# A graph network on one core: the second convolution for the two chosen experts only, rows ordered by expert

## The chip, the core and the metric

The kernel runs on one core of a Trainium2 chip. The metric is device time in microseconds (us), measured over whole executions. The profile is one execution recorded by the hardware profiler. In it TensorE is PE (its weight loads PEld), VectorE is DVE, ScalarE is ACT, GpSimd is POOL, and SyncE is SP, which only issues DMAs. Lines such as L1417 are lines of the kernel before.

## What is computed

A graph of N = 10,000 nodes with 512 features has E = 160,000 edges, sorted by destination. Layer 0 is a mixture of four experts, each made of two graph convolutions. Layer 1 is graph attention with a feed-forward part. The change is in layer 0, cut here to what matters:

```python
gates = softmax(x @ gate_W + gate_b)
top_v, top_i = top_k(gates, 2)                  # two of four experts for each node
def sage_conv(h, W_l, b_l, W_r):
    aggr = segment_sum(h[src], dst) * inv_deg   # mean over the incoming edges
    return aggr @ W_l + b_l + h @ W_r
for e in range(4):
    h = x
    for l in range(2):
        h = relu(sage_conv(h, Wl[e, l], bl[e, l], Wr[e, l]))
    expert_outs.append(h)
out = sum(take_along_axis(stack(expert_outs), top_i) * top_v)
x = layernorm(x + out)                          # then layer 1: q, k, v, attention, feed-forward
```

A node uses only the outputs of its two chosen experts, but a node's first convolution is needed for any expert that one of its neighbours along an edge has chosen.

## The kernel before, in words

Nodes are cut into 79 blocks of 128, and a block into four windows of 32 destinations. Each window has 5 slots of 128 edges (`CAP` 5), so a block has 20 gathers. A gather is an indirect DMA that POOL issues: one row of a table for each of 128 edges. PE adds the rows up with a one-hot matrix, 32 destination columns at a time, four windows side by side. A round is one slot of all four windows.

**Stage 1** (72 to 3992 us of the span) takes the blocks in pairs. `gather` sums the rows of `x`; `turned` transposes sums and own rows; `conv` (L1181 to L1191) computes the first convolution of all four experts with the weights held still and 256 nodes streaming; `products` (L1193 to L1203) multiplies the result at once with the second convolution's `Wl` (`wn`) and stores it, four experts in eight places a row, in `y_tab`. The eight places hold every pair of experts side by side, so that one gather later brings both chosen rows (1,024 numbers). The activations themselves go to `h_tab`.

Beside that, `side` drives two generators. `plan_src`, on DVE, works out where each edge goes in a table sorted by source for layer 1: 158 counting steps, 158 scanning steps (L969 to L972) and some closing ones. `scatter_src` then sends the edges there, 1,250 indirect DMAs from POOL (L1057). Stage 1's order on PE, DVE, ACT and POOL is written out by hand, so each of these engines does its instructions in the order of the code.

**Stage 2** (3992 to 6991) takes the blocks one by one. `pull` (L1319 to L1326) gathers the pairs of rows into a ring of 12 tiles (`YB`, the tiles `ring` and `y`). `rounds` sums them into two PSUM tiles `p_ag`, one for each chosen expert (L1417). `own` (L1368) multiplies the block's activations with `Wr` of all four experts, adds the bias with a bf16 product of ones and rows, and picks with masks (L1378 to L1385). The two are joined, passed through Relu with the gate as scale, and added to `x`; then come the norm and `project`, which makes q, k and v (L1340). Four and three scatters of the edge table stand in each block. PE and POOL are ordered by hand here, the other engines by the scheduler.

**Stage 3** (6991 to the end) is attention and feed-forward.

A last check adds up flags in `fail`; where one is set (too many edges in a window, for example), a slow general version runs instead.

Of the kernel before, what the change touches and what calls it, by code (L numbers as in the profile page):

```python
# [8 lines left out]
F32 = mybir.dt.float32  # L9
# [611 lines left out]

SPREAD = 60.0
# [12 lines left out]
def fast(ctx: ExitStack, tc: tile.TileContext, a: dict, out: bass.AP, bad: bass.AP):  # L635
# [23 lines left out]
    NPR = NW // 2  # L659
    assert E % P == 0 and E >= SL and NP <= SKIP_ROW and NPR <= 256  # L660

# [14 lines left out]
    fail = consts.tile([P, 4], F32, name="fail")  # L676
# [7 lines left out]
    y_tab = dram.tile([NP, NS, D], F32, name="y_tab")  # L684
    h_tab = dram.tile([NSB, P, NE, KD, 2 * P], F32, name="h_tab")
# [3 lines left out]
    wqkv_s = dram.tile([3, P, KD, D], F32, name="wqkv_s")  # L689
    fold_s = dram.tile([3, D], F32, name="fold_s")  # L690
    rows_s = dram.tile([3, NE + 5, D], BF16, name="rows_s")
# [23 lines left out]
    def split_rows(full, mine, part, i, v, add):  # L715

        nc.sync.dma_start(full, bass.AP(tensor=v.tensor, offset=v.offset, ap=[[0, 3], [1, D]]))
        if add is not None:
            nc.sync.dma_start(mine, add.partition_broadcast(3))
            nc.vector.tensor_add(full, full, mine)  # L720
# [20 lines left out]
    def normed(pool, src, name):  # L741
# [9 lines left out]
        t = pool.tile([P, D], F32, name=name)  # L751
# [6 lines left out]
    gate_w = mp.tile([P, NB, NE], F32, name="gate_w")  # L758
# [7 lines left out]
    empty = mp.tile([P, FC, WP], F32, name="empty")  # L766

    def fill_slots():
        nc.gpsimd.memset(empty, 0.0)
        nc.gpsimd.memset(empty.bitcast(I32)[:, :, 0:1], SKIP_ROW)  # L770
        nc.gpsimd.memset(empty[:, :, 1:2], FAR)
        yield
        for c0 in range(0, NC, FC):
            n = min(FC, NC - c0)
            nc.sync.dma_start(slots1[:, c0:c0 + n, :], empty[:, :n, :])
            yield
# [3 lines left out]
    wn = [wp.tile([P, KD, D], F32, name=f"wn{e}") for e in range(NE)]  # L780
    wr = big[4:7] + [wp.tile([P, KD, D], F32, name="wr3")]
    wl = big[:4]
    nc.gpsimd.memset(ring, 0.0)
# [5 lines left out]
    for w, n in zip(wn, "qkv"):  # L789
        load_to(w, a[f"L1_gnn_W{n}_T"], nc.scalar)  # L790
# [3 lines left out]
    def fold(pool, ps):  # L794
        off = pool.tile([1, D], F32, name="off")
        for i, w in enumerate(wn[:3]):
# [8 lines left out]
            nc.scalar.dma_start(wqkv_s[i], w)  # L805
# [80 lines left out]
    bl = wp.tile([P, NE, KD], F32, name="bl")  # L886
    for e in range(NE):
        nc.sync.dma_start(bl[:, e, :], a["L0_gnn_bl"][e, 0].rearrange("(k p) -> p k", p=P))
    for e in range(NE):
        load_to(wn[e], a["L0_gnn_Wl"][e, 1])  # L890
# [173 lines left out]

    def drive(gen, n):
# [4 lines left out]

    at512 = mp.tile([P, NB], F32, name="at512")
    pick = mp.tile([P, 2, NB, NE], F32, name="pick")
    gsel = mp.tile([P, 2, NB], F32, name="gsel")
# [35 lines left out]


    with p1, tc.tile_pool(name="p1k", bufs=1) as kp, tc.tile_pool(name="p1", bufs=2) as dp, \
# [3 lines left out]
        GB = 10  # L1115
        gbuf = [ring[:, i * D:(i + 1) * D] for i in range(GB)]

        def pull(i):

            b, k = divmod(i, BC)  # L1120
            if b < NB:
                c, j = divmod(k, NQ)
                nc.gpsimd.indirect_dma_start(  # L1123
                    out=gbuf[i % GB], out_offset=None, in_=x,
# [13 lines left out]
        def gather(s, rows):  # L1138

            rounds = [(b, c) for b in SB[s] for c in range(CAP)]  # L1140
            for r, (b, c) in enumerate(rounds):
# [4 lines left out]
                for j in range(NQ):  # L1146
                    i = (b * CAP + c) * NQ + j
                    nc.tensor.matmul(p_ag[j * W:(j + 1) * W, :], oh[:, j * CAP + c, :],  # L1148
                                     gbuf[i % GB], start=(c == 0), stop=(c == CAP - 1))
                for j in range(NQ):  # L1150
                    pull((b * CAP + c) * NQ + j + GB)
# [13 lines left out]
                if r % 2:  # L1165
                    yield
# [7 lines left out]
        def turned_all(rows):  # L1174
            tt = dp.tile([P, 2, KD, 2 * P], F32, name="tt", bufs=1)
# [5 lines left out]
        def conv(tt, e, n):  # L1181
            h = dp.tile([P, KD, 2 * P], F32, name="h", bufs=4)
            for f in range(KD):
                ph = pm.tile([P, D], F32, name="mm")
                for i, w in enumerate((wl[e], wr[e])):
                    for k in range(KD):
                        nc.tensor.matmul(ph[:, :n], w[:, k, f * P:(f + 1) * P], tt[:, i, k, :n],  # L1187
                                         start=(i + k == 0), stop=(i == 1 and k == KD - 1))
                nc.scalar.activation(h[:, f, :n], ph[:, :n], AF.Relu, bias=bl[:, e, f:f + 1])  # L1189
                side(e, f)  # L1190
            return h  # L1191

        def products(s, h, e, n):  # L1193
            for i, b in enumerate(SB[s]):
                py = pm.tile([P, D], F32, name="mm")
                for k in range(KD):
                    nc.tensor.matmul(py, h[:, k, i * P:(i + 1) * P], wn[e][:, k, :],  # L1197
                                     start=(k == 0), stop=(k == KD - 1))
                y = dp.tile([P, D], F32, name="y")
                nc.scalar.copy(y, py)  # L1200
                for at in [k for k in range(NS) if SEQ[k] == e]:
                    nc.sync.dma_start(y_tab[b * P:(b + 1) * P, at, :], y)
            nc.sync.dma_start(h_tab[s, :, e, :, :n], h[:, :, :n])  # L1203

        fill = fill_slots()
        plan = plan_src(kp, pm)
        scat = scatter_src(mp)
        planned, planning = [], [0]

        def side(e, f):  # L1210

            if planned:
                drive(scat, 2 if f < KD - 1 else 1)
            elif f < KD - 1 or e % 2:
                counted = planning[0] > NPR
                for _ in range(1 if counted else 4):
# [7 lines left out]
        vectors = [(a["L0_gnn_bl"][e, 1], None) for e in range(NE)] \  # L1224
            + [(a[f"L1_gnn_b{n}"], fold_s[i]) for i, n in enumerate("qkv")] \
# [700 lines left out]
```

## Time and profile before

| | |
|---|---|
| median of 10 runs | 10,061.99 us (10,054.58 to 10,071.37) |
| the profiled execution | 10,060.42 us |
| its span | 10,058.6 us |
| PE busy | 9,435.7 us, 94% |
| POOL busy | 6,876.2 us, 68% |
| DVE busy | 5,289.6 us, 53% |
| ACT busy | 3,010.8 us, 30% |
| first convolution, PE (L1187, first group) | 8,960 instructions |
| `products`, PE (L1197) | 2,528 instructions |
| `own`, PE (L1378) | 2,528 instructions |
| gathers of stage 1 (L1123) | 1,580 |
| gathers of stage 2 (L1323) | 1,580 |
| scatters of the edge table (L1057) | 1,250 |

An fp32 product is two PE instructions in the trace. Busy times of lines that overlap on PE cannot be added; the lengths of stretches in the timeline can. Issuing an ordinary DMA is not counted as busy time of an engine, but an indirect DMA is busy time of POOL while POOL prepares it; the gap in front of it is listed as idle, with what ended it. "issue" there means that the engine waited for nothing the profile shows.

### The profile page before, as it was taken

What the parts mean: (1) busy time and instruction counts of PE and PEld (TensorE: products, weight loads), DVE (VectorE), ACT (ScalarE), POOL (GpSimd) and SP (SyncE); (2) the same over time, 40 slices, a digit from 0 to 9 for tenths busy, and PEclk for the clock granted to TensorE, in tenths of its full rate; (3) what the DMA queues carried; (4) which work ended last, traced back from release to release, by engine and by line L of the source; (5) the groups of instructions that cost most, each with busy time, mean ns of one, the idle gap of its engine ahead of it and who ended that gap; (6) DMA issues with size and microseconds to landing.
All of it is one profiled execution on the core that took longest, in us unless ns stands there. A gap on an engine that the chain in (4) does not pass through costs nothing.

```text
span 10058.6 us, 169077 instructions
## 1 busy us (share of the span) xinstructions
PE 9435.7 (94%) x63887; PEld 5512.0 (55%) x63887; DVE 5289.6 (53%) x8244; ACT 3010.8 (30%) x5827; POOL 6876.2 (68%) x6736
## 2 busy tenths in 40 slices
PE   7999999999999998999999999998888888888888
PEld 4666666666666665333333333333555555555555
DVE  7898891000000012334333443344888888888885
ACT  1111111111111111111111111111566666666665
POOL 5566666777777774777777777776766666666664
PEclk9999999999999999999999999999999999999999
DMA  6544455455554554888888888886788877887874
GB/s 212 178 154 157 158 160 161 155 161 156 164 167 153 162 156 145 274 293 293 293 296 299 291 293 301 292 296 227 252 255 256 255 250 256 254 254 253 255 256 129
DMA packets 1076313, 2256.12 MB, mean 224 GB/s; under 512 B 250459, under 2 KB 500214, under 8 KB 1074720
## 3 DMA queue, kind: packets, MB, share of 16 engines
q0 software_dynamic: 588224, 1654.56, 51.0%
q1 hardware_dynamic: 479546, 576.99, 17.0%
q10 hardware_dynamic: 7718, 13.65, 0.4%
q8 instruction: 508, 8.32, 0.3%
q14 instruction: 317, 2.60, 0.1%
HBM read 2174.00 MB, written 378.96 MB: 254 GB/s over the span
## 4 chain that ended last, share of the span: by engine, by line
PE 71%; DVE 12%; DMA 8%; ACT 5%; issue 3%; POOL 1%; POOLq 0%; ACTq 0%; DVEq 0%; SPq 0%
PE mm L1187 20%; PE mm L1378 10%; PE mm L1197 10%; PE mm L1340 6%; PE p_ag L1417 6%; PE p_ag L1148 3%; PE bank L1635 3%; DVE s L1853 3%; PE bank L1625 3%; DMA y<-y_tab,ix 3%; DMA kv<-kv_all,meta 2%; PE bank L1585 2%; DVE m L927 2%; ACT L1694 2%; DMA ring<-y_tab,ix 2%
## 5 line engine op out<-in xcount | busy, mean ns | idle before, releaser
L1123 POOL DMA_INDIRECT ring<-in_x_dram,idx_t x1580 | 1896.6, 1200 | 1017.9 <-PE p_ag L1148 573.8
L1187 PE MATMUL mm<-tt,big 128*128 128x256 f32 (+1 forms) x8960 | 1966.9, 378 | 0.0
L1187 PEld LDWEIGHTS mm<-tt,big 128*128 128x128 f32 x8960 | 1682.2, 190 | 290.6 <-issue 70.5
L1057 POOL DMA_INDIRECT sorted<-pay,addr x1250 | 1265.4, 1012 | 380.4 <-issue 329.5
L1543 POOL DMA_INDIRECT kv<-kv_all,meta x948 | 986.7, 1041 | 259.4 <-issue 176.4
L1378 PE MATMUL mm<-big,hb 128*128 128x512 f32 x2528 | 1147.3, 597 | 0.0
L1323 POOL DMA_INDIRECT y<-y_tab,ix x920 | 935.0, 1016 | 307.5 <-issue 182.7
L1197 PE MATMUL mm<-wn,h 128*128 128x512 f32 x2528 | 1124.2, 597 | 0.0
L1189 ACT ACTIVATE h<-mm,bl 128x256 f32<-128x256 f32 (+1 forms) x640 | 301.3, 471 | 2130.3 <-PE mm L1187 2130.3
L1323 POOL DMA_INDIRECT ring<-y_tab,ix x660 | 686.1, 1040 | 274.4 <-issue 136.0
L1703 POOL TENSOR_TENSOR ohp<-oh,p 128x768 f32<-128x768 bf16 x316 | 465.8, 1474 | 585.2 <-ACT p L1694 585.0
L1340 PE MATMUL mm<-big,z_t 128*128 128x512 f32 x1896 | 852.5, 592 | 0.7 <-ACT z_t L1333 0.7
L1197 PEld LDWEIGHTS mm<-wn,h 128*128 128x128 f32 x2528 | 468.7, 190 | 595.2 <-issue 595.0
L1378 PEld LDWEIGHTS mm<-big,hb 128*128 128x128 f32 x2528 | 469.0, 190 | 577.1 <-issue 514.3
L1625 PE MATMUL bank<-big,big 128*128 128x256 f32 (+1 forms) x2560 | 638.8, 394 | 110.1 <-ACT big L1627 105.1
L1385 DVE SCALAR_TENSOR_TENSOR t<-mm,pick,t 128x512 f32<-128x512 f32 x474 | 334.1, 747 | 561.2 <-PE mm L1379 561.0
L1817 DVE TENSOR_TENSOR kv<-qe,kv 128x1024 f32<-128x1024 f32 x474 | 575.8, 1215 | 67.3 <-DMA kv<-kv_all,meta 66.9
L899 DVE TENSOR_TENSOR oh<-loc_t,iota_w 128x640 f32<-128x640 bf16 x158 | 130.3, 826 | 905.9 <-PE p_ag L1148 851.3
L1625 PEld LDWEIGHTS bank<-big,big 128*128 128x128 f32 x2560 | 484.1, 197 | 220.9 <-ACT big L1627 132.8
L1417 PE MATMUL p_ag<-y,oh 128*32 128x512 f32 x3680 | 562.3, 600 | 42.2 <-DMA y<-y_tab,ix 42.0
L1441 ACT ACTIVATE t<-t,gsel 128x512 f32<-128x512 f32 x158 | 109.2, 722 | 1634.1 <-DVE t L1439 1633.9
L1340 PEld LDWEIGHTS mm<-big,z_t 128*128 128x128 f32 x1896 | 360.1, 190 | 425.8 <-issue 417.1
(298 smaller groups left out, 14349.1 us busy)
## 6 DMA issues: line engine op xcount, KB each, us to landing
y_tab<-y SPq DMA_DIRECT2D x632, 256.0 KB
hb<-h_tab SPq DMA_DIRECT2D x316, 256.0 KB
h_tab<-h SPq DMA_DIRECT2D x156, 512.0 KB
kv_all<-kvt SPq DMA_DIRECT2D x79, 516.0 KB
xb<-in_x_dram SPq DMA_DIRECT2D x156, 256.0 KB
q_all<-q SPq DMA_DIRECT2D x79, 384.0 KB
q<-q_all SPq DMA_DIRECT2D x237, 128.0 KB
ring<-in_x_dram,idx_t POOLq DMA_INDIRECT x1580
```

What stands on the lines that cost most here:

```text
L1057: inst = nc.gpsimd.indirect_dma_start(out=sorted1[:], out_offset=bass.IndirectOffsetOnAxis(ap=addr_i[:, c0 + c:c0 + c + 1], axis=0), in_=p ...
L1123: nc.gpsimd.indirect_dma_start(out=gbuf[i % GB], out_offset=None, in_=x, in_offset=bass.IndirectOffsetOnAxis(ap=window(idx_t, b)[:, j, c:c ...
L1187: nc.tensor.matmul(ph[:, :n], w[:, k, f * P:(f + 1) * P], tt[:, i, k, :n], start=(i + k == 0), stop=(i == 1 and k == KD - 1))
L1197: nc.tensor.matmul(py, h[:, k, i * P:(i + 1) * P], wn[e][:, k, :], start=(k == 0), stop=(k == KD - 1))
L1323: nc.gpsimd.indirect_dma_start(out=ybuf[i % YB], out_offset=None, in_=y_flat, in_offset=bass.IndirectOffsetOnAxis(ap=ahead[b][1][:, j, c:c ...
L1340: nc.tensor.matmul(po, z_t[:, k, :], wqkv[i][:, k, :], start=(k == 0), stop=False)
L1378: nc.tensor.matmul(pr, hb[:, k, :], wr[e][:, k, :], start=(k == 0), stop=False)
L1417: nc.tensor.matmul(p_ag[v][j * W:(j + 1) * W, :], oh[:, j * CAP + c, :], g[:, v * D:(v + 1) * D], start=(c == 0), stop=(c == CAP - 1))
L1543: nc.gpsimd.indirect_dma_start(out=to, out_offset=None, in_=kv_all[:], in_offset=bass.IndirectOffsetOnAxis(ap=blocks[b][0].bitcast(I32)[:, ...
L1625: nc.tensor.matmul(ph, up(f, k), z_t[:, k, :m], start=(k == 0), stop=(k == KD - 1))
L1703: eng.tensor_tensor(ohp[:, c0:c1], oh[:, k + c0:k + c1, 0:1, :] .to_broadcast([P, n, H, W]), p[:, c0:c1, :, None].to_broadcast([P, n, H, W ...
L1817: nc.vector.tensor_tensor(k, qe.pop((w, g)), k, op=ALU.mult)
```

## The change

The second convolution is done only for the two chosen experts of each node, after the sum over edges instead of before it.

- Stage 1 computes the first convolution with the nodes held still and the weights streaming (512 columns), one unit for one expert and one block. The bias is added by DVE, Relu follows on ACT, and the activations themselves are stored in the table with eight places (now `h_tab`). `products` and the separate store of activations are gone. `side` runs once after each unit, with 5 counting steps, 1 or 2 scanning steps, or 2 or 3 scatters.
- `places` works out, from the gates, a row for each node and chosen expert in a table ordered by expert, for groups of blocks (three, three, then five each, and three at the end). An expert has room for 256 or 384 rows of a group. A fifth flag tells of an overflow.
- Stage 2 is a chain over three steps. In one step `sum_round` sums the pairs of activations of a group, gathers the block's own two activation rows (`own_i`), and `send` writes sum and own row into `by_exp` with an indirect DMA. One step later `experts` loads those rows in order, transposes them, multiplies with `Wl` and `Wr` of their expert, adds the bias, applies Relu and stores them in `done_s`. One step later still, `nodes` fetches each node's two rows back with indirect DMAs, weighs them with the gates, and does the norms and the projections. The pieces of the three are put in order by fractions of a step.
- The ring of gathered tiles has 6 places instead of 12. Scatters of the edge table are spread over all rounds that are left. The biases of the projections are added by DVE instead of by a product on PE.

```diff
-        YB = 12
+        YB = 6
+        def send():
+            while unsorted:
+                b = unsorted.pop()
+                g = group[b]
+                for v in range(2):
+                    inst = nc.gpsimd.indirect_dma_start(
+                        out=by_exp[g % 3][:], out_offset=row_at(pos_i[:, v, b:b + 1]),
+                        in_=both[:, v, :], in_offset=None, ...)
...
+        def sum_round(b, c):
+            if c == 0:
+                sums[b] = [pa.tile([P, D], F32, name="p_ag") for _ in range(2)]
+            oh = edges[b][0]
+            for v in range(2):
+                for j in range(NQ):
+                    y = ybuf[((b * CAP + c) * NQ + j) % YB]
+                    nc.tensor.matmul(sums[b][v][j * W:(j + 1) * W, :], oh[:, j * CAP + c, :],
+                                     y[:, v * D:(v + 1) * D], start=(c == 0), stop=(c == CAP - 1))
+            for j in range(NQ):
+                pull((b * CAP + c) * NQ + j + YB)
+            if c == 0:
+                send()
+            if c == 1 and b + 1 < NB:
+                edges[b + 1] = fetch(b + 1)
+            if c == 2:
+                for v in range(2):
+                    nc.gpsimd.indirect_dma_start(out=both[:, v, D:], out_offset=None, in_=h_rows,
+                        in_offset=row_at(own_i[:, v, b:b + 1]), ...)
+            scatter(-(-unsent[0] // max(CAP * (NB - b) - c, 1)))
+            if c == CAP - 1:
+                for v, p in enumerate(sums.pop(b)):
+                    nc.scalar.activation(both[:, v, :D], p, AF.Copy, scale=inv_deg[:, b:b + 1])
+                unsorted.append(b)
+        def experts(g):
+            units = [(e, e * GR[g] + r) for e in range(NE) for r in range(0, GR[g], P)]
...
+            load(0)
+            turn(0)
+            yield
+            for u, (e, r) in enumerate(units):
+                turn(u + 1)
+                pr = pm.tile([P, D], F32, name="mm")
+                for i, (t, w) in enumerate(zip(turned.pop(u), (wl[e], wr[e]))):
+                    for k in range(KD):
+                        nc.tensor.matmul(pr, t[:, k, :], w[:, k, :], start=(i + k == 0),
+                                         stop=(i == 1 and k == KD - 1))
+                res = dp.tile([P, D], F32, name="res")
+                nc.vector.tensor_add(res, pr, bias[:, e, :])
+                nc.scalar.activation(res, res, AF.Relu)
+                nc.sync.dma_start(done_s[g % 3][r:r + P, :], res)
...
+        def nodes(b):
+            xb = load_x(dp, b)
+            for v in range(2):
+                nc.gpsimd.indirect_dma_start(out=back[:, v, :], out_offset=None,
+                    in_=done_s[group[b] % 3][:NE * GR[group[b]], :],
+                    in_offset=row_at(pos_i[:, v, b:b + 1]), ...)
...
+            for step in range(NG + 2):
+                todo = []
+                if step < NG:
+                    rounds = [(b, c) for b in GB[step] for c in range(CAP)]
+                    todo += [((i + 0.5) / len(rounds), lambda b=b, c=c: sum_round(b, c))
+                             for i, (b, c) in enumerate(rounds)]
+                if 0 <= step - 1 < NG:
+                    gen = experts(step - 1)
+                    n = NE * GR[step - 1] // P
+                    todo += [(0.12 if i < 0 else 0.16 + 0.84 * (i + 0.5) / n,
+                              lambda gen=gen: next(gen, 1)) for i in range(-1, n)]
...
```

In stage 1:

```diff
-        def products(s, h, e, n):
...
+        def conv(tt, e, i, b):
+            ph = pm.tile([P, D], F32, name="mm")
+            for j, w in enumerate((wl[e], wr[e])):
                 for k in range(KD):
+                    nc.tensor.matmul(ph, tt[:, j, k, i * P:(i + 1) * P], w[:, k, :],
+                                     start=(j + k == 0), stop=(j == 1 and k == KD - 1))
+            y = dp.tile([P, D], F32, name="y", bufs=4)
+            nc.vector.tensor_add(y, ph, bl[:, e, :])
+            nc.scalar.activation(y, y, AF.Relu)
+            for at in [k for k in range(NS) if SEQ[k] == e]:
+                nc.sync.dma_start(h_tab[b * P:(b + 1) * P, at, :], y)
...
+        def side(u):
             if planned:
-                drive(scat, 2 if f < KD - 1 else 1)
-            elif f < KD - 1 or e % 2:
+                scatter(3 if u % 2 else 2)
+            else:
                 counted = planning[0] > NPR
-                for _ in range(1 if counted else 4):
+                for _ in range((2 if u % 4 == 3 else 1) if counted else 5):
...
+                if s < 3:
+                    for r in range(0, NE * max(GR), P):
+                        nc.sync.dma_start(by_exp[s][r:r + P, :], zero)
```

## The prediction

> **What bounds the kernel now.** I read the windows of the three stages first, since the span hides different limits.
>
> ```profile
> 390.00:1478.00 1088.00, 1088.00 (x4886) 744.58 (x4885) 978.74 (x645) 173.71 (x335) 714.61 (x448) 1.00 0.49 156
> 1565.00:3890.00 2325.00, 2304.88 (x10326) 1576.39 (x10325) 200.32 (x491) 368.31 (x710) 1644.09 (x1735) 0.99 0.50 156
> 3992.00:6991.00 2999.00, 2920.81 (x11773) 1153.48 (x11771) 1176.45 (x2173) 518.97 (x870) 2221.37 (x2252) 0.99 0.85 289
> 6991.00:10058.00 3067.00, 2620.44 (x34700) 1713.31 (x34700) 2576.93 (x4365) 1862.74 (x3745) 2018.33 (x2054) 0.97 0.77 243
> ```
>
> Columns: stretch, length, busy PE, PEld, DVE, ACT, POOL (instructions), clock, DMA share, GB/s. PE looks like the bound of stage 1 (72 to 3992) and stage 2 (3992 to 6991). POOL, at 71 to 74%, looks free. It isn't: its gaps must be read, in the groups of 390:1478, of 1565:3890, and of 4100:6900 (three lines).
>
> ```profile
> L1123 POOL DMA_INDIRECT ring<-in_x_dram,idx_t x448 | 716.0, 1598 | 373.7 <-PE p_ag L1148 254.8 <-issue 98.4 <-PE mm L1187 9.4
> ...
> L1123 POOL DMA_INDIRECT ring<-in_x_dram,idx_t x943 | 950.5, 1008 | 454.4 <-issue 230.5 <-PE p_ag L1148 179.6 <-PE mm L1197 12.2
> ...
> L1323 POOL DMA_INDIRECT y<-y_tab,ix x875 | 890.1, 1017 | 292.7 <-issue 171.2 <-PE p_ag L1417 58.3 <-PE mm L1378 12.6
> L1323 POOL DMA_INDIRECT ring<-y_tab,ix x629 | 654.2, 1040 | 243.8 <-issue 128.4 <-PE p_ag L1417 73.8 <-DMA y<-y_tab,ix 11.0
> L1057 POOL DMA_INDIRECT sorted<-pay,addr x527 | 541.6, 1028 | 160.0 <-issue 131.8 <-DMA y<-y_tab,ix 12.2 <-POOL pay L1055 9.0
> ```
>
> Most of that idle time is "issue", 0.30 us each. The timeline shows it ahead of every indirect DMA, however ready:
>
> ```profile
> 6003.54 1.04 POOL L1057 DMA_INDIRECT sorted<-pay,addr  x1 [0.30 <-issue]
> 6004.89 1.01 POOL L1057 DMA_INDIRECT sorted<-pay,addr  x1 [0.31 <-issue]
> 6006.21 0.98 POOL L1057 DMA_INDIRECT sorted<-pay,addr  x1 [0.30 <-issue]
> ```
>
> So one indirect DMA costs POOL about 1.31 us. In 4100:6900 the 2,031 of them, at 1.028 + 0.30 + 0.01 for the payload copies = 1.34, fill 2,720 of 2,800 us. Stage 2 has 27 a block: 36.2 us, and a block takes 36.3 there. PE's part is 35.05, so both are full. In the scan part of stage 1 (390:1478) a gather takes 1.598 beside the long DVE scans, 1.90 with the gap.
>
> How long a pull takes to land, I read where stage 2 starts with little in flight (POOL, then PE):
>
> ```profile
> 4035.76 0.99 POOL L1323 DMA_INDIRECT ring<-y_tab,ix  x1 [17.44 <-PE p_ag L1417]
> 4037.06 0.99 POOL L1323 DMA_INDIRECT ring<-y_tab,ix  x1 [0.30 <-issue]
> ...
> 4040.12 1.04 PE L1417 MATMUL p_ag<-ring,oh 128*32 128x512 f32 x2 [0.76 <-DMA ring<-y_tab,ix]
> 4042.38 1.05 PE L1417 MATMUL p_ag<-ring,oh 128*32 128x512 f32 x2 [1.22 <-DMA ring<-y_tab,ix]
> ```
>
> That is 4.4 and 5.3 us from issue to use. In a busy stretch the same reading gives 9 to 10 (issued 5555.07, used 5564.18).
>
> **Stage 1.** PE loses `products`: 2,528 instructions. Eight of them run in 3.43 us, 0.43 each: 1,085 us, 13.7 a block. The convolution turned round streams as many columns (8 instructions of 256 take 1.73 us, so 16 of 512 take 6.9). A block falls from 48.6 to about 34.8 us. That is the gain if nothing else binds. But:
>
> - Counting, 5 steps a unit (a unit: one expert on one block), 4 units a block: DVE 20 x 1.505, plus 4 new bias additions of 0.69, plus one-hot, slots and small ones 2.6 = 35.5. 32 units, 8 blocks at 36, plus 25 for the slow first block: 313 us.
> - Scanning: 158 steps, 1.25 a unit, 126 units, 31.6 blocks. POOL: 20 gathers at 1.90 = 38.0, over DVE's 5 x 5.95 + 5.4 = 35.2 and PE's 34.8. 1,200 us. If the gathers hide, 1,100.
> - Rest of the plan: 14 units, 3.5 blocks at 36: 126.
> - Scattering, 10 a block: POOL 30 x 1.31 + 0.5 for copies = 39.7, over PE. 136 units, 34 blocks: 1,350.
> - Last pair, no gathers: 8 units of 7 us, 56. `places` puts two PE products behind the gates, and some 150 small DVE instructions of 0.15 to 0.2 us: 30 to 60, say 45. Sum 101. If hidden under the convolutions, nothing.
>
> Sum 3,090 against 3,890 (102 to 3992): **800 saved, not 1,085**. ACT exchanges Relu of 256 (0.471) and copies (0.585) for Relu of 512 (0.72), and is 16% busy: nothing, and 0 to 20 if DVE lags behind four PSUM tiles. SP loses the `h` stores; the 36 zero fills (19 MB, 65 us at 290 GB/s) lie in the first three pairs at half DMA load: nothing, up to 40 without that cover.
>
> The shorter stage 1 gives POOL fewer places for the edge table: in the built order the first scatter follows 910 of 1,580 gathers, and 352 scatters lie in stage 1, against about 697 before. 898 are left for stage 2, against 553.
>
> **Stage 2.** PE: sums 8.7 a block as before (5 rounds of 1.74). `own` (14.6) gives way to 192 units of 16 instructions (6.87) and 8 transposes (0.9): 2.43 a block, 18.9. Projection 10.8. With 0.3 of `fetch`, 38.7 against 35.05.
>
> POOL: 20 pulls, 2 sends, 2 own rows, 2 back, 11.4 scatters: 37.4 a block x 1.34 = **50.1 us, against 36.2**. The bound is POOL. New waits on its queue: sends wait for ACT's copies, own rows for the sends two rounds earlier, back rows for the last unit's store some 18 us earlier. All are placed later than the 6 to 10 us that a transfer takes, so nothing; if one store is late, every pull behind it waits, 5 us a group, 85.
>
> The ring falls from 12 tiles to 6. A round uses 4, so two pulls of the next round can only be issued once this one has released their tiles. Chain from round to round: 0.3 release + 1.34 to the second pull + landing + 1.3 last products. Landing between 4.4 and 10; I take 6.5, nearest to the row with few in flight. Chain 9.4.
>
> - Rounds with 2 scatters (57 blocks): three light ones need 6 x 1.34 = 8.0 of POOL, so 9.4 binds; two heavy ones (sends, own rows) 10.7; back rows add 1.9 of 2.7: 51.5 a block, 2,936.
> - Rounds with 3 (the first 22 blocks, the remainder divided by rounds left and rounded up): 3 x 9.4 + 2 x 12.1 + 1.9 = 54.3: 1,195.
> - In the built order of the five-block steps 67 of 350 rounds follow 11 to 12 us of other PE work, which holds POOL's next pulls back some 2.5 us each: 170.
> - Start 11 as before (3992 to 4003). Tail, with no rounds left: 8 units 62, 5 projections 54, three single node chains of about 26: 195.
>
> Sum 4,507 against 2,999: **1,508 more**. DMA moves 13.8 MB a block for 10.8 (rows out, in, out and back again), 260 GB/s at 53 us, under the 289 of before: nothing by itself, but it feeds the landing time. SP issues 4 `hb` loads less and 4.9 row loads and 2.4 stores more a block, at 0.3 to 0.4 us each: some 1.3 us more on a queue that waits most of the time, nothing; if it came ahead of POOL's back rows, 1.3 a block, 100. DVE (1,176 of 2,999) and ACT lose the selection and gain additions of like size: hidden.
>
> Stage 3 is untouched: 3,067.
>
> Total 102 + 3,090 + 4,507 + 3,067 = 10,766 against a span of 10,058.6. The profiled execution took 10,060.42, 1.6 under the median of 10,061.99; I forecast **10,768**, 7% slower.
>
> [...] The row says 4.4 to 5.3 with little in flight, and 9 to 10 with much.
>
> **Rivals.**
>
> - *Landing takes 9.5, not 6.5.* For it: 9.1 and 10.0 in the busy stretch. Against: at most 6 pulls are in flight, not 12. Chain 12.4, every round at least that: 79 x 62 + 170 + 206 = 5,274, total 11,530. At a landing of 8: about 11,080.
> - *Latency hidden, POOL alone.* Landing 4.4 or 5.5: 79 x 50.1 + 206 + part of the 170 = 4,170 to 4,340, and stage 1 up to 100 less: 10,350 to 10,600.
> - *Not slower: an indirect DMA costs POOL less.* Stage 2 may grow by the 800 saved: (3,799 - 206 - 170) / 79 = 43.3 us a block, 1.16 us for each of 37.4. Below that the change breaks even. With PE alone as bound, 10,059 - 1,085 + 79 x 3.7 = 9,270 to 9,300. For it: PE is 97% busy in both stages. Against: 0.98 + 0.30 = 1.28 is the fastest of back-to-back rows in any stage.
> - *It doesn't do what it says*: a group overflows its room and the slow general version runs. Counted from the reference's gates, the fullest expert has 353 of 384 rows, 217 of 256 in a group of three. Excluded.
>
> **Numbers.** My case (landing 5.5 to 8) 0.62, long landing 0.14, POOL alone 0.14, not slower 0.08, no change 0.02. Leaving out half of each outer case and the not-slower one: 10,290 to 11,180. The not-slower case gives faster 0.08; within 0.2% (about what a measurement of this kernel can tell from no change) 0.02; slower 0.90.
>
> **What would show it.** Right: the first stage ends near 3,200, with POOL's gaps at 0.30 in its second half; the second has about 53 us a block, PE under 80% busy and waiting for DMA into `ring` and `y`, POOL waiting for `p_ag` between its bursts. Wrong: PE over 90% busy in the second stage, POOL's spacing under 1.2, or `back` and `by_exp` ending POOL's waits.

## The result and the profile after

The changed kernel takes **11,085.02 us** (median of 8 runs, 11,071.34 to 11,098.52) beside 10,056.62 us for the kernel before (28 runs): a ratio of 1.1024, 95% interval [1.1014, 1.1033]. It is 10.2% slower; forecast were 10,768 us and 7%. The profiled execution has a span of 11,075.4 us.

Windows of the changed kernel; the columns are those of the prediction's first fence (stretch, length, PE, PEld, DVE, ACT, POOL, clock, DMA share, GB/s):

```profile
400.00:1690.00 1290.00, 1212.93 (x3968) 499.29 (x3968) 1094.21 (x877) 134.08 (x228) 1000.51 (x653) 0.98 0.54 165
...
1805.00:3169.00 1364.00, 1286.08 (x4096) 518.91 (x4092) 212.78 (x470) 136.66 (x233) 1034.94 (x1069) 0.98 0.53 161
...
3281.00:7804.00 4523.00, 3726.23 (x12880) 1354.53 (x12880) 865.14 (x1691) 695.20 (x1208) 3018.00 (x3091) 0.89 0.71 238
7804.00:8003.00 199.00, 157.31 (x416) 73.54 (x416) 61.90 (x133) 44.26 (x81) 18.13 (x20) 0.89 0.40 132
8003.00:11075.00 3072.00, 2628.37 (x34700) 1720.68 (x34700) 2567.62 (x4364) 1860.59 (x3744) 2016.76 (x2054) 0.97 0.76 243
```

Stage 1 ends at 3,266 instead of 3,992. Stage 2 then lasts to 8,003: 4,737 us instead of 2,999. Nearly all of it is the rounds, from PE's first sum (3,285) to its last (7,804): 4,519 us, where before they took 2,926 (4,034 to 6,959). Two things differ from the old row of stage 2: PE is no longer full (82% busy for 97%), and its granted clock is 0.89 instead of 0.99.

Groups on POOL in the changed kernel: the scan part (500 to 1600), then the rounds (3285 to 7804; two lines):

```profile
L1198 POOL DMA_INDIRECT ring<-in_x_dram,idx_t x557 | 870.0, 1562 | 232.0 <-issue 132.3 <-PE p_ag L1222 81.4 <-PE mm L1259 9.4
...
L1409 POOL DMA_INDIRECT ring<-h_tab,ix x1314 | 1363.1, 1037 | 1004.8 <-PE p_ag L1436 644.4 <-issue 310.4 <-PE pt L1477 22.8
L1069 POOL DMA_INDIRECT sorted<-pay,addr x887 | 892.6, 1006 | 272.3 <-issue 248.9 <-POOL pay L1067 15.1 <-DMA ring<-h_tab,ix 6.4
```

An indirect DMA still costs POOL 1.0 us and 0.30 of issue. The rounds hold 2,920 of them. POOL's busy 3,015 plus 2,920 x 0.30 = 876 make 3,891 us, 86% of the 4,519; in the rounds before, 2,197 and some 2,055 x 0.30 were 96%. The largest other wait is that of `ring` for `p_ag`, 644: POOL has to wait until PE releases a tile. PE in turn waits for tiles to land (3285 to 7804; total, number, longest):

```profile
PE p_ag L1436 <- DMA ring<-h_tab,ix: 623.8, 281, 9.1
PE p_ag L1436 <- DMA y<-h_tab,ix: 68.1, 68, 3.5
PE pt L1533 <- ACT z L761: 54.1, 16, 10.3
```

One round that waits, POOL and then PE, in the timeline of the changed kernel (start, length, what ended the idle time before):

```profile
5521.26 1.26 POOL L1409 DMA_INDIRECT ring<-h_tab,ix  x1 [2.23 <-PE p_ag L1436]
5522.83 0.99 POOL L1409 DMA_INDIRECT y<-h_tab,ix  x1 [0.30 <-issue]
...
5532.97 1.04 POOL L1409 DMA_INDIRECT ring<-h_tab,ix  x1 [3.81 <-PE p_ag L1436]
```

```profile
5526.26 1.92 PE L1436 MATMUL p_ag<-ring,oh 128*32 128x512 f32 x2 [4.40 <-DMA ring<-h_tab,ix]
5530.74 1.06 PE L1436 MATMUL p_ag<-y,oh 128*32 128x512 f32 x1 [2.57 <-DMA y<-h_tab,ix]
...
5531.59 1.06 PE L1436 MATMUL p_ag<-y,oh 128*32 128x512 f32 x1
...
5532.44 1.91 PE L1436 MATMUL p_ag<-y,oh 128*32 128x512 f32 x2
...
5535.22 3.60 PE L1491 MATMUL mm<-big,turned 128*128 128x512 f32 x8
5538.66 3.60 PE L1491 MATMUL mm<-ext,turned 128*128 128x512 f32 x8
5542.18 1.92 PE L1436 MATMUL p_ag<-ring,oh 128*32 128x512 f32 x16
```

This is the chain of the prediction: the second pull is issued at 5522.83 and used at 5530.74. These 7.9 us are longer than most; the mean over such rounds is 5.26 (table below). But the last products run to 5534.3, 3.6 us, and not 1.3. The fourth tile's two products lie on the same strip of 32 columns, and their four records stand one behind the other, 0.85 us apart. The round at 5542.18 has 7.2 us of convolutions ahead of it, finds all its tiles there, and does all eight of its products in 1.92. Windows of these stretches show what else differs (clock is the third number from the end):

```profile
5512.00:5519.00 7.00, 7.00 (x19) 2.98 (x17) 1.53 (x3) 2.09 (x4) 5.48 (x6) 1.00 0.83 281
5526.00:5535.00 9.00, 6.18 (x18) 1.45 (x19) 1.20 (x4) 1.20 (x4) 4.28 (x5) 0.54 0.74 247
5535.00:5542.00 7.00, 7.00 (x20) 3.08 (x18) 0.00 (x0) 1.06 (x2) 5.29 (x6) 1.00 0.87 279
```

After the wait PE works at 0.54 of its clock on average, and it is back at 1.00 in the next window. In the trace the granted clock has only two values, 1.0 and 0.5; here it is 0.5 from 5524.1 to 5534.3.

### The profile page after: what moved, and what is told of

The parts are those of the page before. It is cut to its first block, busy times and chain, and to the rows that moved or that the text cites. A ratio compares the mean times of both kernels' runs of the same rounds, so it can differ in the third digit from the quotient of the medians.

```text
span 11075.4 us, 158361 instructions
## 1 busy us (share of the span) xinstructions
PE 9538.2 (86%) x57706; PEld 4379.0 (40%) x57706; DVE 5200.3 (47%) x8256; ACT 2943.3 (27%) x5621; POOL 7449.8 (67%) x7211
## 5 line engine op out<-in xcount | busy, mean ns | idle before, releaser
L1409 POOL DMA_INDIRECT ring<-h_tab,ix x1317 | 1366.2, 1037 | 1026.7 <-PE p_ag L1436 644.4
L1259 PE MATMUL mm<-big,tt 128*128 128x512 f32 x4424 | 2001.6, 604 | 19.8 <-ACT tt L1245 12.4
L1436 PE MATMUL p_ag<-ring,oh 128*32 128x512 f32 x5268 | 1320.0, 707 | 624.6 <-DMA ring<-h_tab,ix 623.8
L1259 PEld LDWEIGHTS mm<-big,tt 128*128 128x128 f32 x4424 | 824.3, 192 | 1153.0 <-issue 1059.7
L1491 PE MATMUL mm<-big,turned 128*128 128x512 f32 x2688 | 1188.2, 593 | 0.0
L1541 PE MATMUL mm<-ext,z_t 128*128 128x512 f32 x1896 | 883.6, 617 | 23.3 <-ACT z_t L1535 23.3
L1436 PEld LDWEIGHTS p_ag<-ring,oh 128*32 128x32 f32 x5268 | 228.1, 118 | 1471.0 <-DMA ring<-h_tab,ix 1037.7
L1491 PEld LDWEIGHTS mm<-big,turned 128*128 128x128 f32 x2688 | 497.1, 191 | 565.1 <-issue 555.0
L1222 PE MATMUL p_ag<-ring,oh 128*32 128x512 f32 x3160 | 603.2, 615 | 131.3 <-DMA ring<-in_x_dram,idx_t 130.4
L1779 PE MATMUL bank<-big,big 128*128 128x512 f32 x1264 | 589.4, 595 | 1.2 <-ACT big L1753 0.7
L1541 PEld LDWEIGHTS mm<-ext,z_t 128*128 128x128 f32 x1896 | 361.1, 196 | 529.0 <-issue 488.9
```

Of the source, the lines that this page charges most:

```text
L1259: nc.tensor.matmul(ph, tt[:, j, k, i * P:(i + 1) * P], w[:, k, :], start=(j + k == 0), stop=(j == 1 and k == KD - 1))
L1409: nc.gpsimd.indirect_dma_start(out=ybuf[i % YB], out_offset=None, in_=h_flat, in_offset=bass.IndirectOffsetOnAxis(ap=edges[b][1][:, j, c:c ...
L1436: nc.tensor.matmul(sums[b][v][j * W:(j + 1) * W, :], oh[:, j * CAP + c, :], y[:, v * D:(v + 1) * D], start=(c == 0), stop=(c == CAP - 1))
L1491: nc.tensor.matmul(pr, t[:, k, :], w[:, k, :], start=(i + k == 0), stop=(i == 1 and k == KD - 1))
L1541: nc.tensor.matmul(po, z_t[:, k, :], wqkv[i][:, k, :], start=(k == 0), stop=(k == KD - 1))
L1779: nc.tensor.matmul(po, hid[:, k, i * P:(i + 1) * P], w2[k // KD][:, k % KD, :], start=(k == 0), stop=False)
```

## The experiments

Four theories of stage 2. **P**: POOL's issue time for 37.4 indirect DMAs a block. **R**: the ring of 6, whose chain from release to release lifts the rounds above that. **C**: PE's clock, low after waits, lengthens this chain. **N**, formed on the way: a node's chain (its pulls, normalisation, transposition) doesn't fit the place that the program order gives it. Expectations count on a chip where the kernel before takes some 10,060 us. "The rounds" are always PE's first sum of stage 2 to its last.

### The kernel before with a ring of 6

```diff
-        YB = 12
+        YB = 6
```

> The kernel before with its ring of pulled tiles cut from 12 to 6 and nothing else changed: same products, same 27 indirect DMAs a block. Theory R (a ring of 6 lets two of a round's four pulls be issued only after the round before has released its tiles, so that each round costs release + second pull + landing + sum, about 10 us): three of the five rounds of a block have no other PE work before them and wait, some 3 x 10 + 14.6 of own convolutions + 10.8 of projection, 50 to 57 us a block for 36.3; stage 2 of 3,950 to 4,500 for 2,999, total 11,000 to 11,550. Theory P (only the number of POOL's indirect DMAs counts): 10,060 to 10,160.

Measured: 11,668.23 us, ratio 1.1588 [1.1569, 1.1608]. Windows of the rounds, of the kernel before and of this run:

```profile
4034.00:6959.00 2925.00, 2856.14 (x11619) 1125.18 (x11611) 1147.85 (x2121) 510.16 (x855) 2196.58 (x2222) 1.00 0.85 291
4036.00:8577.00 4541.00, 3616.02 (x11620) 1243.33 (x11621) 1145.00 (x2121) 510.06 (x855) 2194.26 (x2234) 0.87 0.59 188
```

2,925 became 4,541 us, with the same POOL work (2,194 busy for 2,197) and the same PE instructions. So a short ring alone can cost 1,616 us: R exists, and the time lies 118 us above the top of my range for it. It also shows C's symptom: the clock fell from 1.00 to 0.87, and the same instructions take PE 3,616 us for 2,856. The older kernel has its rounds in groups of three and two with nothing between them, which may be why it suffers more from 6 tiles than the changed one (next run).

### The changed kernel with a ring of 10

Holding one projection matrix for q, k and v gives the room.

```diff
-    ext = [mp.tile([P, KD, D], F32, name=f"ext{i}") for i in range(4)]
+    ext = [mp.tile([P, KD, D], F32, name=f"ext{i}") for i in range(2)]
-    wqkv = ext[1:]
+    wqkv = [ext[1]] * 3
-        YB = 6
+        YB = 10
```

> The changed kernel with a ring of 10 tiles. Room for it comes from holding one projection matrix instead of three: q, k and v are all computed with the last one loaded, so those outputs are not the reference's; the instructions are the same. Theory R+P (the ring lifts the rounds above POOL's issue time, 37.4 x 1.34 = 50.1 us a block): the rounds fall from 4,523 to 3,960 to 4,100 us, PE no longer waits for DMA in most rounds, total 10,510 to 10,660. If the ring is not what holds the rounds (landing or traffic whatever the ring): 0 to 100 less than the changed kernel, 10,985 to 11,085.

Measured: 10,828.65 us, ratio 1.0760 [1.0742, 1.0778]. The rounds took 4,252 us, 267 less than with 6 tiles. That is about half of what R+P expected (423 to 563): the ring counts, but POOL's issue time isn't reached. PE's waits (rounds of this kernel; total, number, longest) show what came in its place:

```profile
PE pt L1533 <- ACT z L761: 338.4, 52, 11.2
PE p_ag L1436 <- DMA ring<-h_tab,ix: 167.2, 88, 10.8
PE p_ag L1436 <- DMA y<-h_tab,ix: 91.9, 80, 4.8
```

PE's wait for pulled tiles, `ring` and `y` together, fell from 692 to 259 us. The transposition's wait for the normalised node `z`, 54 us in the changed kernel, rose to 338.

### Scatters of the edge table after stage 2

```diff
             if planned:
-                scatter(3 if u % 2 else 2)
+                pass
...
-            scatter(-(-unsent[0] // max(CAP * (NB - b) - c, 1)))
```

> The changed kernel, ring of 6, with all 1,250 scatters of the edge table sent after stage 2 instead of beside stages 1 and 2. At the end they cost 1,250 x 1.31 = 1,640 us. Stage 1: its last 34 blocks should fall from POOL's 39.7 to PE's 34.8 us, 170 less (if PE were the bound there: 0). Stage 2, theory P alone (POOL's issue sets the rounds): 11.4 x 1.34 = 15 us a block less, 1,200 less, total 11,350. Theory R (the ring's chain sets them): five chains of 10.5 to 11 us a block are left, the rounds fall from 4,523 only to 4,150 to 4,350, total 12,180 to 12,390.

Measured: 12,357.63 us, ratio 1.2276 [1.2256, 1.2297], in R's range. Windows of the rounds and of stage 1's last 34 blocks:

```profile
3147.00:7492.00 4345.00, 3672.74 (x12880) 1354.28 (x12880) 856.27 (x1637) 692.37 (x1208) 2070.78 (x2033) 0.91 0.72 245
1805.00:3010.00 1205.00, 1187.16 (x4073) 502.88 (x4072) 207.42 (x444) 137.56 (x236) 671.49 (x668) 0.99 0.59 180
```

887 scatters left the rounds, 1,160 us of POOL's time at 1.31; the rounds lost 174. With a ring of 6, then, POOL's issue isn't what holds most of them. In stage 1 it is: the same PE work took 1,205 instead of 1,364 us, 159 less (expected 170), and PE now fills 98.5% of it.

### Both: ring of 10 and scatters after stage 2

The edit is the sum of the last two.

> Both: ring of 10 (q, k and v all computed with one projection matrix, so not the reference's values there) and all edge-table scatters after stage 2. Theory R+P: with neither the ring nor the scatters, PE's 38.7 us a block binds (POOL 26 x 1.34 = 34.8), the rounds take 3,060 to 3,320 us, total 11,080 to 11,340. If transfers set the floor (13.8 MB a block at the 289 GB/s that the kernel before reached is 47.7 us): rounds 3,700 to 3,800, total about 11,750. If the ring chain is not what holds e3: as e3.

Measured: 11,998.3 us, ratio 1.1928 [1.1908, 1.1948]. The rounds took 3,977 us, far over the 3,320 expected. PE's waits in them:

```profile
PE pt L1532 <- ACT z L761: 264.9, 40, 9.8
PE pt L1476 <- DMA rows<-by_exp: 160.2, 17, 13.3
PE pt L1476 <- DVE mp L1393: 66.9, 28, 4.9
```

With neither ring nor POOL in the way, PE is busy 3,334 us at a clock of 0.91, and of the 643 us in which it stands still the largest part, 265, is the wait for `z`. The program places a node's transposition 0.09 of a step after its pulls: 2.25 of 25 rounds, 22 us when a round takes 10. I had put a single node's chain at about 26 us. That is theory N.

### The same with a node's PE steps later

```diff
-                                 for d in (0.0, 0.03, 0.09, 0.11, 0.13, 0.15)]
+                                 for d in (0.0, 0.03, 0.15, 0.17, 0.19, 0.21)]
```

> The kernel with ring of 10 and scatters last, and a node's PE steps placed 0.06 of a step later (0.15, 0.17, 0.19, 0.21 for 0.09, 0.11, 0.13, 0.15), 3.75 rounds behind the node's two pulls instead of 2.25. q, k and v again with one projection matrix. In the run without this, the rounds took 3,977 us against PE's 3,060, and PE's transposition waited 265 us for the normalised node. Theory N (the single node's chain of about 26 us no longer fits into 2.25 rounds of 10 us, so that the program order makes PE wait): this wait goes, the rounds fall to 3,680 to 3,760, total 11,700 to 11,790, a ratio of 1.163 to 1.172. If PE then waits as long for rows or tiles that transfers bring: 3,930 to 3,980, total as before, 11,950 to 12,000.

Measured: 11,617.92 us, ratio 1.1545 [1.1527, 1.1562]. Window of the rounds:

```profile
3147.00:6747.00 3600.00, 3223.52 (x12872) 1291.73 (x12870) 838.67 (x1634) 692.00 (x1205) 2070.59 (x2033) 0.96 0.83 296
```

377 us less, more than N expected (217 to 297). The wait for `z` is gone (265 us); the others changed too, but together by little. The clock rose from 0.91 to 0.96, and PE's busy time for the same products fell from 3,334 to 3,224. In the trace PE is busy for 412 us at half clock without the edit and for 185 with it; half of the difference, 114, is about the 110. So here a removed wait gave back its own length and some of the clock's.

### Ring of 8, with all three projections

```diff
-        YB = 6
+        YB = 8
-                        t = dp.tile([P, D], F32, name="rows", bufs=3)
+                        t = dp.tile([P, D], F32, name="rows", bufs=2)
-                res = dp.tile([P, D], F32, name="res")
+                res = dp.tile([P, D], F32, name="res", bufs=1)
-            pay = pool.tile([P, GS, WP], F32, name="pay", bufs=3)
+            pay = pool.tile([P, GS, WP], F32, name="pay", bufs=2)
-            xb = load_x(dp, b)
+            xb = load_x(dp, b, 1)
```

> The changed kernel with a ring of 8 tiles and all its values right: room from one buffer fewer of rows (3 to 2), of res, of the node's x tile (2 to 1) and of the payload (3 to 2). Theory R+P: with 8 tiles a whole round can be pulled ahead, so the rounds come down to POOL's issue time, 3,960 to 4,150 for 4,523; total 10,510 to 10,710. If the ring is not the cause, or a buffer taken away becomes a new wait: 10,950 to 11,150.

This run, with the first tries of the last two experiments below, was on a chip where the kernel before took 10,900.19 us (17 runs). It took 11,657.8 us there, ratio 1.0717 [1.0683, 1.0751]. The changed kernel was not run on that chip, so the ratio says nothing precise of the ring; I ran it again.

> The changed kernel with a ring of 8 and all its values right, once more, since the chip of the first time took 10,900 us for the kernel before. With ring 10 the rounds fell from 4,519 to 4,252. Theory R: 8 tiles hold a whole round ahead, the gain is nearly that of 10: total 10,820 to 10,910, a ratio of 1.076 to 1.085. If the buffers taken away (rows 3 to 2, res, x and payload) cost more than the ring brings: 1.10 or more.

Measured: 10,847.45 us, ratio 1.0774 [1.0758, 1.0791]; the kernel before took 10,063.29. Window of the rounds:

```profile
3301.00:7586.00 4285.00, 3563.18 (x12880) 1360.65 (x12880) 857.86 (x1691) 691.41 (x1207) 3008.85 (x3088) 0.92 0.75 251
```

The rounds took 4,285 us: 8 tiles bring 234 of the 267 that 10 bring, as R says. What the buffers taken away cost isn't separated from this; the total lies in R's range.

### Ring of 8 and a node's PE steps later

The edit is that of ring 8 and that of the later steps.

> The changed kernel with all its values right, ring of 8, scatters in their place, and a node's PE steps 0.06 of a step later. Theory N + P (ring and node steps held the rounds above POOL's issue time, and behind them that issue time binds): PE's wait for the normalised node, 264 us with ring 8, goes, and the rounds fall from 4,285 to POOL's 37.4 x 1.34 x 79 = 3,960 or little over it, 3,960 to 4,080, though they took 3,601 with ring 10, late steps and no scatters; total 10,520 to 10,650, a ratio of 1.045 to 1.058. If POOL's issue is no floor: rounds under 3,900, total under 10,470. If another wait takes the node's place: 4,230 or more, a ratio of 1.072 or more.

Measured: 10,659.94 us, ratio 1.0588 [1.0570, 1.0605], 10 us over the range. Window of the rounds:

```profile
3296.00:7393.00 4097.00, 3527.24 (x12873) 1340.03 (x12872) 848.03 (x1688) 692.65 (x1205) 3010.88 (x3088) 0.94 0.77 262
```

POOL's waits in 3289 to 7300, the largest three:

```profile
POOL sorted L1069 <- issue: 223.1, 723, 1.7
POOL ring L1409 <- issue: 206.3, 666, 2.4
POOL ring L1409 <- PE p_ag L1436: 191.3, 120, 6.8
```

The rounds fell by 188 to 4,097 us, 497 more than in the run without scatters beside them (which had two tiles more; in the unmoved order these brought 33). PE's wait for `z` went from 264 to 0.4 us, but that for `mp`, with which DVE works out the next block's pulls, rose from 8 to 153. POOL's 3,011 busy and 876 of issue are 95% of the rounds. So with ring and node steps mended POOL's indirect DMAs fill the rounds nearly alone, as P says, at 51.9 us a block against the 37.0 of the kernel before. No run took the scatters off this very version; that they bind there is read from the 95% and from the 497.

### Keeping PE's clock up

The first try put 16 products of zero weights on one strip of 32 columns ahead of each round.

```diff
+            for k in range(16):
+                nc.tensor.matmul(sums[b][0][:W, :], nought, wl[k % 4][:, k // 4, :],
+                                 start=(c == 0 and k == 0), stop=False)
```

> The changed kernel with 16 more products ahead of every round's sums: a zero weight against columns already in SBUF, added into the same sum, so the values stay as they are. They need no transfer, take 1.74 us at the full clock and lie in PE's waiting time. Theory C (PE's granted clock, 0.89 on average in stage 2, falls while it waits for pulls, and the slower sums and convolutions lengthen the chain from round to round): the clock rises to 0.96 or more, a round's eight products come back from 2.8 towards 1.9 us, the rounds fall by 150 to 350 from 4,523; total 10,740 to 10,940. If the clock is only a consequence of the waiting: 0 to 200 more, 11,085 to 11,290.

Measured: 15,318.31 us, ratio 1.4078 [1.4037, 1.4120], on the slower chip. The experiment was mis-made. PE's group in 4000 to 8000:

```profile
L1436 PE MATMUL p_ag<-big,nought 128*32 128x512 f32 x5963 | 2593.0, 593 | 0.0
```

One product has two records (6,320 for the 3,160 of the changed kernel's sums), so 2,593 us for 2,981 products is 0.87 us each, 13.9 us a round, where I had counted 1.74. On one strip they run one after the other; a round's own eight lie on four strips, two on each, and take 1.74 to 1.92 together. The second try spread them over the strips and put them where PE waits.

```diff
                 for j in range(NQ):
                     y = ybuf[((b * CAP + c) * NQ + j) % YB]
+                    for k in range(16 if v == 0 and j == 2 else 0):
+                        q = k % NQ
+                        nc.tensor.matmul(sums[b][1][q * W:(q + 1) * W, :], nought,
+                                         wl[q][:, k // NQ, :], start=(c == 0 and k < NQ), stop=False)
```

> The changed kernel, ring of 6, with 16 products of zero weights put into every round just where PE waits, ahead of the round's third pulled tile. They lie on all four column strips, as the round's own products do, so they take 1.74 us at the full clock; they add zero, and the values stay. Theory C (PE's granted clock, 0.90 in the rounds, is low because PE waits, and slow products and convolutions between the rounds make the chain longer): the clock of the rounds rises to 0.96 or more and the rounds fall by 150 to 350 from 4,519; total 10,740 to 10,940, a ratio of 1.067 to 1.088 to the kernel before. If the low clock costs nothing that the waiting does not hide: 0 to 140 us more, a ratio of 1.102 to 1.117.

Measured: 11,699.41 us, ratio 1.1626 [1.1608, 1.1644], outside both ranges. Sixteen products took some 3.6 us instead of 1.74: eight take 1.74, and I had halved the price. Window of its rounds, and PE's group of sums in 3290 to 8300:

```profile
3290.00:8427.00 5137.00, 4727.64 (x25520) 1758.45 (x25520) 867.80 (x1691) 700.40 (x1208) 3019.23 (x3089) 0.98 0.64 209
```

```profile
L1442 PE MATMUL p_ag<-ring,oh 128*32 128x512 f32 x5176 | 1287.5, 617 | 243.3 <-DMA ring<-h_tab,ix 242.6
```

The clock did come back, 0.90 to 0.98, and a record of the sums is 617 ns for 707. What that does to the chain is read from the rounds that follow the round before directly (within 0.5 us, so that nothing but the chain sets them), as means over them, from the trace:

| rounds that follow directly | changed | scatters last | zero products |
|---|---|---|---|
| number | 109 | 116 | 114 |
| release to the second pull's start, us | 1.89 | 1.25 | 2.24 |
| that pull to the last waited product, us | 5.26 | 5.31 | 5.56 |
| the rest of the sums, us | 3.51 | 3.35 | 2.25 |
| the round, us | 10.67 | 9.91 | 10.05 |

With the clock kept up, the rest of the sums takes 1.3 us less, and the round is shorter though 3.6 us of products were put into its wait. The total rose by some 600 us all the same: the same products also stand in rounds that don't wait, some 18 us of PE's time a block, and the rounds grew by 7.8 a block. So it is shown for these rounds that the low clock follows from the waits and lengthens the chain. What it is worth in the total isn't shown, since no run kept the clock up for nothing. The traces give an estimate of its direct part: in the rounds of the changed kernel the clock is at 0.5 for 949 of the 4,519 us, and PE is busy for 686 of these (19 in the kernel before). In the round shown above the records on one strip follow 0.85 us apart, at half clock; in the first try, at a clock of 0.98, 0.43. If all that work gains so, it would take some 340 us less at the full clock. A mean clock alone would mislead here, since it also counts time in which PE waits: with a ring of 10 it is 0.89, as low as with 6, but PE is busy at half clock for 459 us only.

### The kernel before with more scatters in stage 1

Its stage 2 was full on POOL (96% of the rounds) and PE (2,856 of 2,925 us) at once, and the second part of its stage 1 on PE alone (2,305 of 2,325 us).

```diff
-                drive(scat, 2 if f < KD - 1 else 1)
+                drive(scat, 2)
...
-                drive(scat, 4)
+                drive(scat, 3)
```

> The kernel before, with eight scatters of the edge table instead of seven beside each expert of a pair in stage 1 (16 a block for 14), and six instead of seven a block in stage 2. Stage 1's second part has PE at 48.6 us a block and POOL at 34 x 1.31 = 44.8, which becomes 47.5: still under PE. Stage 2 has POOL at 36.2 and PE at 35.05 a block: POOL becomes 34.9. If POOL's issue sets stage 2 by that small margin, 60 to 95 less: 9,960 to 10,000. If PE sets it: 10,050 to 10,060. If stage 1 turns to POOL: more than 10,070.

On the slower chip: 10,879.63 us, ratio 0.9988 [0.9969, 1.0007], no difference clear of noise.

> The kernel before with 16 scatters a block for 14 in stage 1 and six for seven in stage 2, once more on another chip if one is given. Stage 2 by POOL's margin: 60 to 95 less, a ratio of 0.991 to 0.994. If PE sets stage 2: 0.999 to 1.000.

Measured: 10,011.6 us beside 10,063.29, ratio **0.9946** [0.9933, 0.9960]. Window of its rounds:

```profile
4045.00:6905.00 2860.00, 2816.57 (x11620) 1124.44 (x11613) 1146.16 (x2115) 510.18 (x855) 2102.80 (x2111) 1.00 0.87 297
```

96 scatters left the rounds (456 for 552): 2,860 us for 2,926, and PE is now 98.5% busy. Stage 1 grew by 11. The gain, 52 us, is a little under the 60 to 95 expected. Small as it is (0.5%), this version is the fastest of all, with two numbers changed.

## Why the prediction was right, and where it wasn't

The sign and the mechanism held: PE's saving came, and POOL with a short ring took more than it. Of the signs named ahead, the end of stage 1 (3,266), POOL's gaps of 0.30, PE's wait for `ring` and `y` (692 us) and POOL's for `p_ag` came; a block took 57 us for 53, and PE was 82% busy, not under 80%. Forecast and measurement, for the profiled execution:

| step | forecast | measured |
|---|---|---|
| counting, with the head | 415 | 400 |
| scanning | 1,200 | 1,290 |
| rest of plan | 126 | 115 |
| scattering | 1,350 | 1,364 |
| last pair | 101 | 97 |
| start of stage 2 | 11 | 19 |
| rounds | 4,301 | 4,519 |
| tail | 195 | 199 |
| stage 3 | 3,067 | 3,072 |
| span | 10,766 | 11,075 |

- **Stage 1**: 726 us saved for 800. The step that was mis-sized is "20 gathers at 1.90": beside the DVE scans a gather took 1.562 + 0.417 = 1.98, 39.6 us a block; part of the gap is POOL waiting for PE's sums (81 us of 232). That three engines were within 10% of each other is the likely reason; no run tested it. That POOL and not PE binds the scattering part was shown by taking the scatters away.
- **The rounds, 218 us too few.** The step that failed is "Chain 9.4", and in it two terms, in opposite directions. "1.3 last products" measured 3.51 us. The fourth tile's two products lie on one strip, where a product took 0.87 us (first try of the zero products), so 1.74 was the least to count, and 2.25 was measured with the clock kept up; the rest is PE's half clock after a wait. "Landing 6.5" measured 5.26. The release and second pull, 1.64, took 1.89. Together they make the 10.67. On the 109 rounds that the chain alone sets, 1.27 us more is at most 140 of the 218; the rest must lie in the other rounds (next point). The total came out where the long-landing rival puts "a landing of 8", but that is chance: landing was shorter than forecast, not longer.
- **"67 of 350 rounds follow 11 to 12 us of other PE work"**: 172 of 393 rounds found all their tiles (their sums took under 1.95 us), with 10.06 us since the round before, nearly all of it other PE work, and took 11.98 us each. Rounds are held either by PE's own work or by the chain. I had given most rounds POOL's or the chain's price. PE's work itself was under-counted: it was busy 3,726 us in the rounds, where the forecast's 79 x 38.7 = 3,057, less the 116 that it puts behind the last round, are 2,941. Its sums alone took 1,416 us, for 79 x 8.7 = 687 in the forecast and 829 in the kernel before. One record of a sum took 707 ns for 599, 18% longer, so the clock is the smaller part of that. A round that waits does its products tile by tile, as in the timeline above, and not on four strips at once.
- **"The bound is POOL", 50.1 us a block**: not yet at this size. POOL was 86% occupied, and taking 887 scatters off gained only 174 us. It nearly becomes the bound, at 51.9 us a block, with ring 8 and later node steps. Of the 1,593 us that the rounds grew, 234 are the ring (6 to 8), 188 the node steps, and 1,171 remain with POOL 95% occupied; the 10.4 more indirect DMAs a block at 1.34 us make 1,101. The "36.3" that a block of the kernel before takes was low, too: 2,926 us are 37.0 a block. No term of the sum rests on it.
- **"All are placed later than the 6 to 10 us that a transfer takes, so nothing"**: true for POOL, whose waits before `by_exp`, `both` and `back` were 0.3 us at most in the rounds. But a node's chain (pulls, normalisation, transposition) holds more than one transfer, and its wait stood on PE, which the forecast didn't look at. It cost 54 us as the change stands, and 264 to 338 where the rounds were shorter and the node steps in their old place.
- **Landing and the clock**: the pulls that the chain waits for took 5.26 us, within the 4.4 to 5.3 read with little in flight and under the 6.5 that I took, and the shorter landing was outweighed by the last products. The clock I had left out: it was 0.54 in the window behind a wait of 4.40 us, and 1.00 in those before the wait and after. The kernel before, with 69 us of PE's waits for pulled tiles in its rounds, kept 0.99 to 1.00 and did not show it.
- **Rivals**: "POOL alone" gave 10,350 to 10,600; with the ring and the node steps mended the kernel took 10,660, so it was close to the right floor, but not of this kernel. "Not slower" fell with 1.31 us for each indirect DMA. Stage 3 and the tail took what was forecast.

**Open**: how much of the total the low clock is worth beyond the estimate of some 340 us of PE's time; whether the traffic of 238 to 296 GB/s lengthens the landings, and by how much, since no run varied it by itself; and what holds the rounds at 3,600 us with ring 10, no scatters and later steps, where the forecast's work of PE at full clock is 2,941 (it waits 145 us for `rows`, 112 for `mp`, 109 for pulled tiles, at 0.96 of the clock and 296 GB/s).

## What to carry to other kernels

Count the engine that issues indirect DMAs like a compute engine, issue gap included: here 10.4 more indirect DMAs a block, 13.9 us at 1.34 each, are as much as the 13.7 us of PE work saved, of which only 9.2 came (726 us / 79). When a buffer ring is halved, time the whole chain from release to release, and price the work behind a wait at PE's low clock (0.54 in the window shown) and tile by tile (3.51 us for the last products, where 1.3 were forecast). When a stage gets faster, look again at every place in a fixed program order that was only just late enough: the next wait stands there.

## What was not expected of the hardware

- PE's granted clock was 0.54 in a 9 us window that starts at the end of a wait of 4.4 us and holds one of 2.6, and 1.00 in the 7 us behind it; over all rounds of the changed kernel 0.90. The last products of a waiting round took 3.51 us, and 2.25 with the clock kept up.
- Sixteen 128x512 products on one 32-column strip took 13.9 us; spread over the four strips, some 3.6.
- One of the chips took 10,900 us for the kernel before, 8% more than the others, at a granted clock of 0.97 for 0.98. What differs there wasn't looked into; comparisons hold only on one chip.
